# Binarised convolution, linear attention and a top-2 expert layer on one core: roots begun on ScalarE, 456 sorted chunks, a shorter Gram chain and more spread buffers

## The chip, the cores and the metric

The kernel runs on one core of a Trainium2 chip. A core has TensorE (PE in the profile; PEld are its weight loads), VectorE (DVE), ScalarE (ACT), GpSimd (POOL) and SyncE (SP), each with its own in-order stream of instructions, and 16 DMA engines that move data between device memory and the on-chip SBUF. The metric is device time of one execution, in microseconds (us), as the median of several executions.

## What is computed

The input x is 32 images of 128 channels and 56 x 56 pixels, so 3136 tokens of 128 numbers an image. Cut to what matters:

```python
# layer 0: group norm, signs, 3x3 convolution with signs as weights, scaled by channel
x = x + conv(sign(gn(x)), sign(w)) * Alpha          # w from M, Z, rv
# layer 1, on tokens t = x as (image, 3136, 128)
n = layernorm(t)
q, k, v = n @ Wq + bq, n @ Wk + bk, n @ Wv + bv
t = t + q * sum_over_tokens(k * v)                  # one row of 128 per image
n = layernorm(t)
p = softmax(n @ router_w + router_b)                # 8 experts
w1, w2 = the two largest of p, divided by their sum
t = t + w1 * (n @ E[e1] + b[e1]) + w2 * (n @ E[e2] + b[e2])
```

## The kernel before

**Tiles.** An image is 25 chunks of 128 tokens (the last has 64); four chunks are a block, so 7 blocks. x lies by channel (128 partitions x 3136) in one of three buffers `x_all`, and by token in one of three buffers `tok_all`. Convolution is nine bf16 matmuls for eight rows (L642). `to_tokens` (L667) turns it to tokens. `stats` (L682, L893) gives the sums for the variances, `var_of` and `rstd_of` (L507 to L527) the roots 1/sqrt(var) of all 25 chunks at once as a 128 x 25 tile: an integer shift and a subtraction from a constant make the first guess, and `NEWTON = 3` rounds of three DVE instructions refine it. This is done twice per image, for `r1` and `r2`.

**Attention.** sum(k * v) follows from the Gram matrix of the normalised tokens. `scaled` (ACT) and `gram` (PE, L744) build it with one more column, the sum of the tokens. Then a chain of eight steps goes back and forth: `kv_1` PE, `kv_2` DVE (three instructions), `kv_3` PE, `kv_4` DVE, `kv_5` PE (a one-column product that turns the row kv into a column), `kv_6` DVE, `kv_7` PE, `kv_8` ACT. Their results are the matrix `move` and the bias, which `project` (L863) and `bias` (L815) need.

**Experts, dense.** For a dense block the kernel computes all eight experts. The gates of the tokens (zero for six of eight) go to device memory (`gate_store`) and come back spread over 128 partitions: `spread` (L1132) loads two experts' gates for a block, 512 KB, into one of four `bc` buffers. `gated` (L1141) multiplies the turned tokens by them on DVE, and `experts` (L1159) sums the products on PE, two f32 matmuls for a `gated`. `finish` and `store` follow.

**Experts, sorted.** For the other chunks only the two chosen experts are computed. Images form groups; `GROUPS = (8, 8, 8, 4)` gives the groups' sizes and `DENSE = (8, 8, 12, 12)` the number of an image's chunks that stay dense; the last four images are dense throughout. That makes 428 sorted chunks. Each token has one of 28 pairs of experts. `pair_of` and `places` count, within the group, how many tokens of the pair came before, with the group's count so far carried as two bf16 rows `count_h` and added by two one-row matmuls (L1281). `scatter` (POOL, L1365) writes each row of a chunk to its place. When the group is complete, `list_1` to `list_4` make the list of tiles of 128 rows with one pair each. Four tiles are a quad: `tile_load` (SP), `tile_turn` (L1669), `tile_experts` (L1687, with the experts' columns from registers), `tile_read` (ACT, L1705 and L1712), `tile_sum`, `tile_out`, `tile_store`. Then `gather` (POOL, L1444) fetches rows back by token, `back_turn` (L1459), `back_out` (ACT, L1467, into one of two `o` buffers) and `back_store` (SP, L1471) finish them.

**Order.** Each step is entered with `at(due, key, engine, work, do, after, take, free, delay)`: a due time, its engine, an estimated cost, what it must follow, and which rings of buffers it takes and frees. `in_order` simulates the engines with these costs and picks, among the steps that can start soonest on an engine, the one with the earliest due time. An image begins every `P = 60` planned us. `TILE_PACE` sets over how many images' time a group's quads are due, `GATHER_PACE` the same for its gathers. The program is then emitted in that order, and each engine runs its share in it. SP issues nearly all transfers in one queue: spreads, tile loads, stores and the loads of x.

The lines that say where a spread lands before the change:

```python
bc = bpool.tile([C, 2, WIDE], F32, tag="bc", bufs=4, name=f"bc_{i}_{b}_{k}")
nc.sync.dma_start(
    bc[:, :, :n],
    d["gp"][b, 2 * k : 2 * k + 2, :n].unsqueeze(0).to_broadcast([C, 2, n]),
)
```

Of the kernel before, what the change touches and what calls it, by code (L numbers as in the profile page):

```python
# [54 lines left out]
C = 128  # L55
# [13 lines left out]
GROUPS = (8, 8, 8, 4)  # L69
DENSE = (8, 8, 12, 12)  # L70
# [9 lines left out]
NEWTON = 3  # L80
# [4 lines left out]
TILE_PACE = (0.7, 0.6, 0.4, 0.3)  # L85
GATHER_PACE = (1.0, 0.8, 0.5, 0.4)
N_Q = C + 2 * N_EXP
Q_GROUP = 3

# [10 lines left out]
    t_in=3, turned=2, v=3, w=2, back=12, sent=4, o=2,  # L100
# [85 lines left out]
def conv_attn_moe_kernel(  # L186
# [63 lines left out]
    one_i = const.tile([C, 1], I32, name="one_i")  # L250
    nc.vector.memset(one_i, 1)
    guess = const.tile([C, 1], I32, name="guess")
    nc.vector.memset(guess, 0x5F3759DF)
# [64 lines left out]
    for j in range((K_REP + 1) // 2):  # L318
        flat = tok_all[j].rearrange("p c e -> p (c e)")
        z_sb += [flat[:, : TAPS * C], flat[:, TAPS * C : 2 * TAPS * C]]  # L320
    for k in range(2):
        load_x(0, nc.sync, k, 2)
# [37 lines left out]
    wv_bk = const.tile([C, C], F32, name="wv_bk")  # L360
    n_bkbv = const.tile([C, C], F32, name="n_bkbv")
# [5 lines left out]
    def prepare():  # L367
# [25 lines left out]

        nc.vector.tensor_mul(wv_bk, wv_sb, bk_bc)
        nc.vector.scalar_tensor_tensor(
            n_bkbv, bk_bc, float(n_tok), bv_bc, ALU.mult, ALU.mult
        )

# [30 lines left out]
    count_h = const.tile([C, 2, N_PAIR], BF16, name="count_h")  # L429
# [5 lines left out]
    def prepare_sorted():  # L435
        nc.gpsimd.memset(hot_all, 0.0)
        nc.vector.memset(count_h, 0.0)
# [68 lines left out]

    def rstd_of(var, dst, name):  # L507

        square = spool.tile([C, n_ck], F32, tag=f"square{name}", bufs=1, name="square")
        shape = [C, n_ck]  # L510
        nc.vector.tensor_tensor(
            square.bitcast(I32),
            var.bitcast(I32),
            one_i.to_broadcast(shape),
            ALU.logical_shift_right,
        )
        yield
        nc.vector.tensor_tensor(
            dst.bitcast(I32), guess.to_broadcast(shape), square.bitcast(I32), ALU.subtract
        )  # L520
        for _ in range(NEWTON):
            yield
            nc.vector.tensor_mul(square, dst, dst)
            yield
            nc.vector.scalar_tensor_tensor(square, square, -0.5, var, ALU.mult, ALU.mult)
            yield
            nc.vector.scalar_tensor_tensor(dst, square, 1.5, dst, ALU.add, ALU.mult)  # L527

    def sent_from(i, g):
# [5 lines left out]
        return [("scatter", i, c) for c in blocks[g]]  # L535

# [7 lines left out]
    def plan_image(i: int):  # L544
# [144 lines left out]

        def rstd1():  # L690
            yield from rstd_of(d["var1"], d["r1"], "1")
# [34 lines left out]
        at(s + 44, ("rstd1", i), "DVE", [0.10] * (2 + 3 * NEWTON), rstd1, after=[("var1", i)])  # L726
# [33 lines left out]
        def kv_2():  # L760
            tok_sum = d["g_sb"][:, C : C + 1]
            prod = spool.tile([C, C], F32, tag="prod", bufs=1, name=f"prod_{i}")
            nc.vector.scalar_tensor_tensor(prod, bv_bc, tok_sum, d["gv"], ALU.mult, ALU.add)
            yield
            nc.vector.tensor_mul(prod, prod, wk_sb)
            yield
            nc.vector.scalar_tensor_tensor(prod, wv_bk, tok_sum, prod, ALU.mult, ALU.add)
            d["prod"] = prod

        def kv_3():  # L770
            d["kv_ps"] = ps_acc.tile([C, C], F32, tag="acc", name=f"kv_ps_{i}")
            nc.tensor.matmul(d["kv_ps"], lhsT=ones, rhs=d["prod"], start=True, stop=True)

        def kv_4():

            kv = spool.tile([C, C], F32, tag="prod", bufs=1, name=f"kv_{i}")
            nc.vector.tensor_add(kv, n_bkbv, d["kv_ps"])
# [4 lines left out]
            d["kv"] = kv  # L782

        def kv_5():
            d["kvc"] = ps_acc.tile([C, 1], F32, tag="acc", name=f"kvc_ps_{i}")
            nc.tensor.matmul(d["kvc"], lhsT=d["kv"], rhs=ident[:, :1], start=True, stop=True)
# [1091 lines left out]
```

## Time and profile before

| what | us |
|---|---|
| median of three runs (2252.52, 2253.8, 2270.36) | 2253.8 |
| the profiled execution's own time | 2270.18 |
| its span, first to last instruction | 2268.4 |
| PE busy | 2103.4 |
| DVE busy | 1970.1 |
| ACT busy | 1531.2 |
| POOL busy | 1041.1 |

The mean granted clock of PE was 0.975, the DMA engines moved 198 GB/s on average. Busy time is the time in which an engine had at least one instruction under way; matmuls overlap, so a busy PE isn't PE at its best pace. A line of a group of instructions names line, engine and operation, then what is written and read, the count, and after the bar the busy time and the mean duration in ns, then the idle time of the engine just before these instructions with what ended it. In the chain of waits each line has its start, its length and what the end of the run was waiting for. An f32 matmul shows as two records of PE, so the 384 units of `experts` with two matmuls each are 1536 records.

### The profile page before, as it was taken

The page shows a single profiled execution, that of the slowest core. Times are in us where ns is not written, and L with a number is a line of the kernel's source. Part 1 is how long each engine was busy: PE and PEld are TensorE (multiplying, and loading weights), DVE is VectorE, ACT ScalarE, POOL GpSimd, SP SyncE. Part 2 cuts the span into 40 slices and gives each one's busy share as a digit, 9 for nine tenths or more (in the row PEclk, how much of TensorE's full clock was granted, in tenths as well). Part 3 has the DMA queues.
Part 4 walks back from the last instruction along what each step waited for, and adds up shares of the span by engine and source line. Part 5 has one row for each costly group of instructions (what it writes and reads, how often), then busy time and mean ns, then how long its engine had stood idle before and what let it go on. Part 6 is the DMA issues. An engine that isn't in the chain of part 4 may idle for free.

```text
span 2268.4 us, 45320 instructions
## 1 busy us (share of the span) xinstructions
PE 2103.4 (93%) x12074; PEld 1449.1 (64%) x12074; DVE 1970.1 (87%) x6074; ACT 1531.2 (68%) x4917; POOL 1041.1 (46%) x1013
## 2 busy tenths in 40 slices
PE   5899999899999999789999999988999999999888
PEld 2666656557777776457676776655676666676544
DVE  4899999999989999688888889988898798789865
ACT  5667776668888887468777867655877776574311
POOL 3044443333433325466443644676654446233563
PEclk9989999999999999899999999999999999999999
DMA  4155544465665565377667766667767777878788
GB/s 166 30 175 177 167 153 141 138 184 184 203 186 165 176 181 168 110 219 252 194 202 220 226 198 202 215 214 240 225 195 232 217 203 247 249 214 270 222 278 273
DMA packets 324364, 448.58 MB, mean 198 GB/s; under 512 B 61832, under 2 KB 222128, under 8 KB 324112
## 3 DMA queue, kind: packets, MB, share of 16 engines
q1 hardware_dynamic: 294384, 382.80, 54.7%
q0 software_dynamic: 28144, 56.14, 8.2%
q10 hardware_dynamic: 1584, 6.75, 0.8%
q8 instruction: 102, 1.67, 0.3%
q14 instruction: 150, 1.23, 0.2%
HBM read 319.51 MB, written 126.00 MB: 196 GB/s over the span
## 4 chain that ended last, share of the span: by engine, by line
PE 42%; DVE 5%; DMA 3%; issue 2%; ACT 2%; another core or an unknown queue 1%; SPq 0%; POOL 0%; DVEq 0%; ACTq 0%; POOLq 0%
PE ff L1159 14%; PE to L1687 7%; PE cv L642 6%; PE q L863 3%; PE gram L744 3%; PE turn L1669 2%; PE back_ps L1459 2%; PE xt L667 2%; DVE gated L1141 1%; DMA back<-res,res_no 1%; PE l L1114 1%; DMA out_dram<-o 1%; PE ff L1153 1%; DMA bc<-gp 0%
## 5 line engine op out<-in xcount | busy, mean ns | idle before, releaser
L1365 POOL DMA_INDIRECT rows<-tok,row_no x428 | 524.3, 1225 | 570.5 <-ACT tok L1358 235.8
L1159 PE MATMUL ff<-gated,ew_d 128*128 128x512 f32 (+1 forms) x1536 | 711.5, 592 | 23.8 <-DVE gated L1141 19.8
L1444 POOL DMA_INDIRECT back<-res,res_no x428 | 485.4, 1134 | 464.1 <-PE back_ps L1459 264.1
L1141 DVE TENSOR_TENSOR gated<-tt,bc 128x1024 f32<-128x1024 f32 x384 | 450.7, 1180 | 92.2 <-PE ff L1159 29.9
L642 PE MATMUL cv<-xs,w_bin 128*128 128x440 bf16 (+3 forms) x2016 | 429.8, 362 | 18.5 <-ACT xs L599 10.0
L1159 PEld LDWEIGHTS ff<-gated,ew_d 128*128 128x128 f32 x1536 | 274.5, 193 | 258.6 <-issue 202.2
L1705 ACT ACTIVATE v<-to,t_in 128x128 f32<-128x128 f32 x528 | 255.3, 484 | 138.1 <-PE to L1687 74.6
L642 PEld LDWEIGHTS <-w_bin 128*128 128x128 bf16 x2016 | 200.1, 100 | 187.8 <-issue 38.3
L1687 PEld LDWEIGHTS to<-ew_s,turned 128*128 128x128 f32 x2112 | 260.8, 194 | 57.8 <-issue 32.4
L877 ACT ACTIVATE qs<-q,r 128x136 f32<-128x136 f32 (+1 forms) x800 | 247.6, 406 | 70.3 <-PE q L863 35.1
L1687 PE MATMUL to<-ew_s,turned 128*128 x2112 | 273.3, 279 | 18.2 <-ACT turned L1675 8.1
L735 ACT ACTIVATE y<-tok,r 128x128 f32<-128x128 f32 (+1 forms) x800 | 257.0, 428 | 24.3 <-PE gram L744 10.4
L863 PE MATMUL q<-move,x 128*128 128x144 f32 (+1 forms) x1600 | 239.9, 295 | 12.7 <-issue 3.7
L863 PEld LDWEIGHTS q<-move,x 128*128 128x128 f32 (+1 forms) x1600 | 213.6, 193 | 42.4 <-issue 21.1
L744 PEld LDWEIGHTS gram<-y 128*128 128x128 f32 (+1 forms) x1600 | 203.3, 192 | 53.9 <-issue 40.4
L744 PE MATMUL gram<-y 128*128 128x129 f32 (+1 forms) x1600 | 217.8, 281 | 12.9 <-issue 8.1
L682 DVE BATCH_NORM_STATS2 st<-tok 128x6 f32<-128x128 f32 (+1 forms) x800 | 185.4, 279 | 31.9 <-ACT tok L673 26.9
L1712 ACT ACTIVATE w<-to,t_in 128x128 f32<-128x128 f32 x528 | 208.6, 395 | 0.0
L893 DVE BATCH_NORM_STATS2 st<-tok 128x6 f32<-128x128 f32 (+1 forms) x800 | 198.1, 284 | 6.3
L673 ACT COPY tok<-xt 128x512 f32<-128x512 f32 (+1 forms) x224 | 121.2, 561 | 99.9 <-PE xt L667 71.6
L653 DVE SCALAR_TENSOR_TENSOR x<-cv,alpha_col,x 128x448 f32<-128x448 f32 x224 | 151.3, 676 | 40.1 <-PE cv L642 7.2
L890 DVE TENSOR_TENSOR tok<-tok,qs 128x408 f32<-128x408 f32 (+1 forms) x288 | 156.1, 542 | 29.4 <-ACT tok L882 24.1
(229 smaller groups left out, 2896.0 us busy)
## 6 DMA issues: line engine op xcount, KB each, us to landing
bc<-gp SPq DMA_DIRECT2D x368, 512.0 KB
x<-in_x_dram SPq DMA_DIRECT2D x116, 392.0 KB
t_in<-rows SPq DMA_DIRECT2D x528, 66.0 KB
res<-v SPq DMA_DIRECT2D x132, 256.0 KB
out_dram<-o SPq DMA_DIRECT2D x100, 256.0 KB
out_dram<-tt SPq DMA_DIRECT2D x92, 256.0 KB
rows<-zeros SPq DMA_DIRECT2D x116, 66.0 KB
rows<-tok,row_no POOLq DMA_INDIRECT x428
```

Of the source, the lines that this page charges most:

```text
L642: nc.tensor.matmul(cv[:, r0:r1, c0:c1], lhsT=w_bin[:, t, :], rhs=xs[:, b * ROWS + dy + r0 : b * ROWS + dy + r1, dx + c0 : dx + c1], start= ...
L735: nc.scalar.mul(y[:n, j, :C], d["tok"][:n, c, :C], d["r1"][:n, c : c + 1])
L744: nc.tensor.matmul(d["gram"], lhsT=y[:n, j, :C], rhs=y[:n, j, :], start=(c == 0), stop=(c == n_ck - 1),)
L863: nc.tensor.matmul(p[:n, k, :], lhsT=d["x"][:, c * C : c * C + n], rhs=move, start=True, stop=True,)
L877: nc.scalar.mul(qs[:n, k, :], p[:n, k, : C + N_EXP], d["r1"][:n, c : c + 1])
L1141: nc.vector.tensor_tensor(g[:, :, :n], d["tt", b][:, :n].unsqueeze(1).to_broadcast([C, 2, n]), d.pop(("bc", b, k))[:, :, :n], ALU.mult,)
L1159: nc.tensor.matmul(d["ff", b][:, :n], lhsT=ew_d[:, e * C : (e + 1) * C], rhs=g[:, j, :n], start=False, stop=(e == N_EXP - 1),)
L1365: dma = nc.gpsimd.indirect_dma_start(out=groups[group]["rows"], out_offset=bass.IndirectOffsetOnAxis(ap=d["row_no"][:n, c - n_dense : c - ...
L1444: dma = nc.gpsimd.indirect_dma_start(out=d["back", c][:n, :], out_offset=None, in_=groups[group]["res"][: quads_of(group) * WIDE, :], in_o ...
L1687: nc.tensor.matmul(p[:, k, j, :], lhsT=t[:, n * C : (n + 1) * C], rhs=ew_s[:, bass.ds(d["cols", q][j][n], C)], start=True, stop=True,)
L1705: nc.scalar.activation(d["v", q][:, n, :], p[:, k, 0, :], AF.Identity, bias=row[:, C + 2 : C + 3], scale=row[:, C : C + 1],)
L1712: nc.scalar.mul(d["w", q][:, n, :], p[:, k, 1, :], row[:, C + 1 : C + 2])
```

## The change

1. `rstd_of` starts from `seed_of`: ScalarE computes exp(-0.5 ln(var)), and one Newton round follows on DVE in place of three. New steps `seed1`, `seed2` stand on ACT between `var` and `rstd`. The set of ACT's functions that has both is loaded at the start.
2. `GROUPS` becomes (8, 8, 7, 5) and `DENSE` (8, 8, 8, 12): images 16 to 22 keep 8 dense chunks instead of 12, image 23 passes to the last group and keeps 12. 456 chunks are sorted, 139 quads instead of 132. `TILE_PACE` becomes (0.8, 0.7, 0.5, 0.4).
3. The two bf16 parts of the count stand in rows 0 and 32 of one tile, with `both` selecting these rows, so that one 33-row matmul adds them.
4. The Gram chain: the terms in the token sum are added by matmuls in `kv_3`, which also makes the column that `kv_5` made; `kv_5` is gone and `kv_6` follows `kv_3` directly.
5. In images 30 and 31 every second spread of a block sequence goes to one of three slots in the x buffer that image 29 used, once its projection is done. They count as a ring of their own, `late`.

```diff
-GROUPS = (8, 8, 8, 4)
-DENSE = (8, 8, 12, 12)
+GROUPS = (8, 8, 7, 5)
+DENSE = (8, 8, 8, 12)
...
-NEWTON = 3
...
-TILE_PACE = (0.7, 0.6, 0.4, 0.3)
+TILE_PACE = (0.8, 0.7, 0.5, 0.4)
...
+LATE, LATE_IN = 30, 29
...
+    nc.scalar.preload_act_table_set("natural_log_exp_and_others")
     for k in range(2):
         load_x(0, nc.sync, k, 2)
     nc.scalar.dma_start(rv_bc, rv.to_broadcast([C, K_REP]))
...
+    def seed_of(var, dst):
+        nc.scalar.activation(dst, var, AF.Ln)
+        nc.scalar.activation(dst, dst, AF.Exp, scale=-0.5)
+
     def rstd_of(var, dst, name):
 
         square = spool.tile([C, n_ck], F32, tag=f"square{name}", bufs=1, name="square")
-        shape = [C, n_ck]
-        nc.vector.tensor_tensor(
-            square.bitcast(I32),
-            var.bitcast(I32),
-            one_i.to_broadcast(shape),
-            ALU.logical_shift_right,
-        )
+        nc.vector.tensor_mul(square, dst, dst)
         yield
-        nc.vector.tensor_tensor(
-            dst.bitcast(I32), guess.to_broadcast(shape), square.bitcast(I32), ALU.subtract
-        )
-        for _ in range(NEWTON):
-            yield
-            nc.vector.tensor_mul(square, dst, dst)
-            yield
-            nc.vector.scalar_tensor_tensor(square, square, -0.5, var, ALU.mult, ALU.mult)
-            yield
-            nc.vector.scalar_tensor_tensor(dst, square, 1.5, dst, ALU.add, ALU.mult)
+        nc.vector.scalar_tensor_tensor(square, square, -0.5, var, ALU.mult, ALU.mult)
+        yield
+        nc.vector.scalar_tensor_tensor(dst, square, 1.5, dst, ALU.add, ALU.mult)
...
+    n_late = n_tok // (2 * WIDE)
+
+    def late_of(i, n):
+
+        turn = n % (2 * n_late + 1)
+        return turn // 2 if i >= LATE and turn % 2 else None
...
-        at(s + 44, ("rstd1", i), "DVE", [0.10] * (2 + 3 * NEWTON), rstd1, after=[("var1", i)])
+        at(s + 43, ("seed1", i), "ACT", 0.45, seed1, after=[("var1", i)])
+        at(s + 44, ("rstd1", i), "DVE", [0.10] * 3, rstd1, after=[("seed1", i)])
...
         def kv_2():
-            tok_sum = d["g_sb"][:, C : C + 1]
-            prod = spool.tile([C, C], F32, tag="prod", bufs=1, name=f"prod_{i}")
-            nc.vector.scalar_tensor_tensor(prod, bv_bc, tok_sum, d["gv"], ALU.mult, ALU.add)
-            yield
-            nc.vector.tensor_mul(prod, prod, wk_sb)
-            yield
-            nc.vector.scalar_tensor_tensor(prod, wv_bk, tok_sum, prod, ALU.mult, ALU.add)
-            d["prod"] = prod
-
-        def kv_3():
-            d["kv_ps"] = ps_acc.tile([C, C], F32, tag="acc", name=f"kv_ps_{i}")
-            nc.tensor.matmul(d["kv_ps"], lhsT=ones, rhs=d["prod"], start=True, stop=True)
+            d["prod"] = spool.tile([C, C], F32, tag="prod", bufs=1, name=f"prod_{i}")
+            nc.vector.tensor_mul(d["prod"], wk_sb, d["gv"])
+
+        def kv_3():
+            p = ps_acc.tile([C, C + 1], F32, tag="acc", name=f"kv_ps_{i}")
+            tok_sum = d["g_sb"][:, C : C + 1]
+            nc.tensor.matmul(
+                p[:, :C], lhsT=tok_sum.to_broadcast([C, C]), rhs=wv_bk, start=True, stop=False
+            )
+            nc.tensor.matmul(p[:, :C], lhsT=ones, rhs=d["prod"], start=False, stop=True)
+            nc.tensor.matmul(p[:, C:], lhsT=d["prod"], rhs=ones[:, :1], start=True, stop=False)
+            nc.tensor.matmul(p[:, C:], lhsT=wv_bk, rhs=tok_sum, start=False, stop=True)
+            d["kv_ps"] = p
...
-        def kv_5():
-            d["kvc"] = ps_acc.tile([C, 1], F32, tag="acc", name=f"kvc_ps_{i}")
-            nc.tensor.matmul(d["kvc"], lhsT=d["kv"], rhs=ident[:, :1], start=True, stop=True)
...
-            bc = bpool.tile([C, 2, WIDE], F32, tag="bc", bufs=4, name=f"bc_{i}_{b}_{k}")
+            slot = late_of(i, b * N_EXP // 2 + k)
+            if slot is None:
+                bc = bpool.tile([C, 2, WIDE], F32, tag="bc", bufs=4, name=f"bc_{i}_{b}_{k}")
+            else:
+                bc = x_all[LATE_IN % HELD][:, slot * 2 * WIDE : (slot + 1) * 2 * WIDE]
+                bc = bc.rearrange("c (j t) -> c j t", j=2)
...
             if not first_of_group:
-                for j in range(2):
-                    nc.tensor.matmul(
-                        p,
-                        lhsT=ones_h[:1],
-                        rhs=count_h[:1, j].unsqueeze(1).to_broadcast([1, n_sort + 1, N_PAIR]),
-                        start=False,
-                        stop=False,
-                    )
+                nc.tensor.matmul(
+                    p,
+                    lhsT=both,
+                    rhs=count_h.unsqueeze(1).to_broadcast([n_part, n_sort + 1, N_PAIR]),
+                    start=False,
+                    stop=False,
+                )
```

The second root (`seed2`, `rstd2`) is changed like the first, and constants are prepared once at the start: `wv_bk` takes in the term in `bv`, `rw_n` the router times the constant part of the column.

## The prediction

> **What bounds the kernel now.** I read the page's busy times first, then a table of busy time by stage, then the timelines of TensorE (PE) and VectorE (DVE), and last the chain at the end of the span.
>
> ```profile
> PE 2103.4 (93%) x12074; PEld 1449.1 (64%) x12074; DVE 1970.1 (87%) x6074; ACT 1531.2 (68%) x4917; POOL 1041.1 (46%) x1013
> L1159 PE MATMUL ff<-gated,ew_d 128*128 128x512 f32 (+1 forms) x1536 | 711.5, 592 | 23.8 <-DVE gated L1141 19.8
> L1141 DVE TENSOR_TENSOR gated<-tt,bc 128x1024 f32<-128x1024 f32 x384 | 450.7, 1180 | 92.2 <-PE ff L1159 29.9
> ```
>
> Two engines are nearly full, so the share alone decides nothing. The stages do (columns: PE, PE weight loads, DVE, ACT, POOL busy with instruction counts, granted clock, DMA share, GB/s):
>
> ```profile
> 100.00:540.00 440.00, 406.75 (x2285) 269.38 (x2284) 427.48 (x1504) 299.82 (x1007) 183.59 (x169) 0.97 0.49 155
> 540.00:900.00 360.00, 353.04 (x2277) 260.40 (x2277) 337.96 (x1065) 304.50 (x995) 136.62 (x110) 1.00 0.60 181
> 900.00:1060.00 160.00, 136.04 (x746) 90.15 (x745) 131.19 (x465) 104.21 (x342) 95.35 (x83) 0.93 0.62 196
> 1060.00:1500.00 440.00, 425.69 (x2552) 302.76 (x2550) 394.17 (x1180) 329.39 (x1057) 224.35 (x190) 0.99 0.70 214
> 1500.00:1560.00 60.00, 49.71 (x246) 30.85 (x245) 46.37 (x172) 28.29 (x92) 41.45 (x38) 0.89 0.56 157
> 1560.00:1900.00 340.00, 318.78 (x1930) 230.96 (x1930) 287.09 (x849) 248.28 (x786) 182.26 (x158) 0.98 0.76 227
> 2100.00:2268.00 168.00, 143.17 (x520) 78.41 (x519) 113.21 (x214) 32.23 (x92) 85.71 (x74) 0.93 0.79 258
> ```
>
> DVE sets the pace up to 540 us (97% busy), PE from 540 to 900 (98%) and mostly to 2100. Around 900 and 1500, where a group of sorted images turns over, and after 2100, no engine is full and PE's clock falls.
>
> Busy matmuls overlap, so I took each PE record's cost from its start to the next start, idle left out. The medians: ff 0.430 us a record (an f32 matmul is two records), to 0.112, 128-wide transposes 0.110, the bias matmul 0.22, kv_ps 0.150, a 504-wide count matmul 0.265. Median times count, over all kinds, is 2004 us of PE work at full pace. The other 264 us of the span are 27 of start, about 138 of gaps, and about 99 of slower records. The same reading prices a small DVE instruction: chained, 0.22 apart; between other work it adds only 0.08.
>
> ```profile
> 919.62 0.19 DVE L511 TENSOR_TENSOR square<-var,one_i 128x25 int32<-128x25 int32 x1
> 919.85 0.19 DVE L518 TENSOR_TENSOR r<-guess,square 128x25 int32<-128x25 int32 x1
> ...
> 911.98 0.17 DVE L525 SCALAR_TENSOR_TENSOR square<-square,var 128x25 f32<-128x25 f32 x1
> 912.06 0.29 DVE L893 BATCH_NORM_STATS2 st<-tok 128x6 f32<-128x128 f32 x1
> ```
>
> Over the run, L523, L525, L527 take 0.156, 0.152, 0.135 each and L511, L518 0.138 and 0.144; that is what I subtract, not their 180 ns of busy time.
>
> **The change, part by part.**
>
> *Roots.* 64 roots lose two integer steps and two of three Newton rounds: 128 x (0.156+0.152+0.135) + 64 x (0.138+0.144) = 74.8 us of DVE, 2.34 per image. They gain two 128x25 activations each. The nearest row is the Exp on ratio (L973, same shape, 226 ns median, 0.172 start to start): 128 x 0.172 = 22 us of ACT, in an engine 68% busy. What the trace does not show is the new trip DVE to ACT to DVE. Its nearest case is the same Exp: DVE's L977 behind it never sat idle for it in 32 cases, while ACT waited for DVE there 1.4 us on average (46.1 in 32). So the lower bound of the added wait is 0 and the upper 64 x 1.4 = 90 us of ACT idle, which matters only between 540 and 900, where ACT is 85% busy: 6 images x 2 x 1.4 = 17 us, with the seeds' own 2 us: 19. I take 3, since the tiles there are also spread out. The seeds also shorten the chain from 11 dependent steps to 5.
>
> The one ACT_TABLE_LOAD, 1.28 us at 8.15, now precedes the weight transfers on ACT's queue, whose sums release the first convolution: 0 to +1.3, I take 1. The changed kernel's instruction list has one table load, as before. The Trainium skill ("ScalarE: Activation LUTs", What ACT_TABLE_LOAD costs) speaks against mixing functions: each switch to another set is about 2.7 us. By that rule, as an estimate, two switches per root would be 128 x 2.7 = 340 us. No run here shows a second load.
>
> *Shorter Gram chain.* DVE's three steps (0.300, 0.243, 0.289) become one of about 0.21: -0.62 per image, 20 us in all. PE loses the one-column kvc matmul and gains a 128-wide and two one-column f32 ones: 0.30 + 0.16 = 0.46 per image, +15 us. One hop PE to DVE to PE disappears; in mid-run other work covers it. It shows where cover is thin: at image 31 PE idles 2.21 before L786. Bounds 0 and -2.2 at each of images 0, 1 and 31; I count it in the tail.
>
> The clock falls with such holes: between 100 and 120 us PE's gaps are at most 2.3 us long and the granted clock is 0.74. The Trainium skill ("TensorE: Matmul & The Clock Gate", What's actually happening) puts the drop to half rate after an idle window of about 3.4 us, by which holes this short should cost only themselves. The trace disagrees.
>
> *Counts.* 48 one-row matmuls become 24: -5 us of PE. A bf16 rest of one row instead of 128 on DVE changes nothing that I can price: 0.
>
> *Seven dense blocks become sorted* (428 to 456 chunks; 528 to 556 tiles, since each group also pads). A dense block costs PE 16 x 0.430 + 0.22 + 4 x 0.110 + 0.11 = 7.65: -53.6. A tile costs 0.110 + 4 x 0.112 = 0.56, so 28 are +15.6; turning 28 chunks back +3.1; wider places +1.5. Net -33 us of PE. DVE: 28 gated products at 1.11 and 7 finishes at 0.6 out, -35; tile sums +9, wider one-hot rows +7: -19. ACT: 28 x (0.346+0.260+0.329) + 3 = +29. POOL: 28 x (1.225+1.134) = +66, with about 95 us of ring waits between 1944 and 2085 to absorb it. SP's transfers: -28 spreads of 512 KB, +28 tile loads and 7 result stores.
>
> *Later tiles.* Group 0's forty quads are asked for over 6.4 images rather than 5.6, so ACT has less per image before 900 and PE something to do after it. In 900 to 1060 PE lacks 24 us; I bound the effect by -15 and +15 and take -3.
>
> *More late slots.* Images 30 and 31 get three more spread buffers. What they address is in the chain at the end:
>
> ```profile
> 2192.32 9.07 another core or an unknown queue
> 2201.43 0.04 issue
> 2201.47 0.59 ACT o L1467
> 2202.08 0.36 SPq L1471
> 2202.44 0.04 issue
> 2202.48 6.24 DMA bc<-gp
> 2208.75 1.24 DVE gated L1141
> ```
>
> ACT waits 9 us for an o buffer, the store behind it blocks SP's in-order queue, and the spread queued behind the store lands 6 us later; the clock in that slice is 0.72. With seven slots the spreads stand earlier on SP. Bound: nothing, or the 15 us from 2192 to 2208; with the Gram chain I take -8 for the tail.
>
> **The sum**, against the profiled execution's own 2270.2 us. To 540: DVE sheds 2.34 + 0.62 = 2.96 for each of nine images, 27; PE, at full pace 373 of the 420 us from 120 to 540, leaves room, but then both engines are tight: -20 (between -27 and 0). Swap, where PE is 94 to 97% busy: -28 of the 33, the rest lost in gaps (between -35 and -15). Gram matmuls less counts after 540: +7. Turnovers -3, ACT waits +3, start +1, tail -8. Total -48, that is 2222. The profiled run lies 16 above the median of the three shown (2253.8); the same difference there gives **2206**.
>
> **Rivals.**
> 1. *PE takes it all back* (about the same). If the stage to 540 is really PE's, with DVE merely running beside it, -20 becomes 0 and the seeds cost ACT 10: -18, so 2236. For it: PE is 92% busy there too. Against it: DVE's starts leave no gap at all from 200 to 400.
> 2. *The gathers at the end* (slower). From 2085 on POOL's gathers run almost without a pause, 1.25 apart, through an o ring of two whose stores land in 5.6 and 6.75 us. If the 28 more chunks all fall there, they cost 28 x 1.25 = 35, and seven more o blocks 7 x 6.75 = 47, a whole landing each as at 2180: +82 in place of -8. With the other terms as they are that gives 2254 - 48 + 90 = 2296. It decides once the last gather comes later than about the middle of image 31's dense blocks. Against it: in the changed order the last turned-back block stands behind image 31's third dense block, one block earlier than before.
> 3. *More comes back than work* (faster still). Holes cost twice, by themselves and by the clock. If a third of the 237 us of gaps and slow records goes with 114 us of DVE work: -79 and -24 of PE work, 2151.
> 4. *Tables are reloaded all the same*: 128 x 1.28 = 164 us on ACT, above 2300. One load in the list speaks against it.
>
> **How the numbers follow.** Forecast 0.60; rival 3 0.15; rival 1 0.14; rival 2 0.10; rival 4 0.01. The predicted time is 2206. A measurement of this kernel tells about 1% from no change (2231 and 2276). Faster 0.75, same 0.15, slower 0.10. The range runs from 2160, which leaves out the lower half of rival 3, to 2255, which leaves out rival 2 and takes in rival 1 and the bad bounds of the first stage and the swap.
>
> **What would show it.** Right: DVE busy about 1820 to 1860 and PE's about 2080; images before 540 us some 2 us closer together; L973-like activations of var at about 0.23 us with no idle on DVE behind them; 340 full-width gated products; no 5 us wait of gated for bc in image 31. Wrong: DVE waiting for r; ACT full from 540 to 900; PE's gaps after 2100 grown beyond 25 us with back on their releasers; a second ACT_TABLE_LOAD.

## The result, and the profile after

The changed kernel took 2284.3 us (median; 2270.3 to 2294.9) against 2262.1 for the kernel before (2252.5 to 2277.9): ratio **1.010**, 95% interval 1.005 to 1.015. It is about 1% slower; 2206 had been forecast. The profiled execution took 2278.9, its span is 2277.2. Here and below, ratios and intervals leave out executions more than 1.5% above the fastest of their kernel, medians don't, and no trace of such an execution (after_again, old_groups_again) is read.

First the page of the changed kernel: busy times and the two groups that were shown of before, then the two activations and the first of the three DVE steps of a root (a line's mean in ns stands after the bar's first number).

```profile
PE 2092.3 (92%) x12224; PEld 1469.9 (65%) x12224; DVE 1875.7 (82%) x5492; ACT 1580.9 (69%) x5136; POOL 1066.6 (47%) x1069
...
L1179 PE MATMUL ff<-gated,ew_d 128*128 128x512 f32 (+1 forms) x1424 | 658.3, 592 | 22.0 <-DVE gated L1161 19.4 <-issue 2.2
...
L1161 DVE TENSOR_TENSOR gated<-tt,bc 128x1024 f32<-128x1024 f32 (+1 forms) x332 | 391.2, 1184 | 134.6 <-PE ff L1179 41.7 <-remote 21.9 <-issue 16.9
```

```profile
L518 ACT ACTIVATE r<-var 128x25 f32<-128x25 f32 x64 | 15.9, 249 | 15.6 <-DVE var L515 14.0 <-issue 1.3 <-DVE gated L1161 0.3
L519 ACT ACTIVATE r<-r 128x25 f32<-128x25 f32 x64 | 14.4, 225 | 2.0
L524 DVE TENSOR_TENSOR square<-r 128x25 f32<-128x25 f32 x64 | 11.7, 182 | 13.8 <-ACT r L519 6.0 <-issue 5.0 <-ACT r L518 2.6
```

The work went nearly as forecast: DVE is busy 94 us less, PE's matmuls at their median pitch sum to 1975 us in place of 1999 (one set of medians for both; the prediction's grouping gave 2004), a seed's two activations take 0.25 and 0.23 us, DVE waits 8.6 us in all for them. What didn't go as forecast is in the stages (columns as in the prediction's table):

```profile
100.00:540.00 440.00, 413.46 (x2390) 281.50 (x2390) 420.77 (x1400) 321.92 (x1088) 186.69 (x177) 0.98 0.50 163
540.00:900.00 360.00, 355.70 (x2324) 265.53 (x2323) 330.06 (x979) 311.97 (x1037) 122.07 (x101) 1.00 0.62 184
900.00:1060.00 160.00, 137.60 (x761) 94.75 (x760) 122.60 (x393) 103.30 (x336) 92.17 (x84) 0.90 0.56 171
1060.00:1500.00 440.00, 401.61 (x2495) 292.29 (x2494) 360.19 (x1104) 330.52 (x1082) 250.65 (x216) 0.95 0.62 185
```

From 1060 to 1500, where PE had been 97% busy at a clock of 0.99, it is 91% busy at 0.95. Counted as PE work still to do, after against before, the changed kernel leads by 37 us at 540, 51 at 1000, 40 at 1300, 32 at 1400, 5 at 1500, and is 18 behind at 2100; 23 of the lead is work that no longer exists. So about 50 us were won by 1000 and lost again, most of it before 1500.

**What PE waits for there.** The timeline of PE in the changed kernel (start, length, what ran, and in brackets the idle time before it with its releaser):

```profile
1038.56 0.27 PE L756 MATMUL gram<-y 128*128 128x129 f32 x1 [0.85 <-issue]
1039.30 0.35 PE L756 MATMUL gram<-y 128*128 128x129 f32 x1 [0.48 <-issue]
1040.70 0.37 PE L756 MATMUL gram<-y 128*128 128x129 f32 x1 [1.05 <-issue]
1042.13 0.38 PE L756 MATMUL gram<-y 128*128 128x129 f32 x1 [1.05 <-issue]
...
1048.47 0.37 PE L1695 MATMUL turn<-ident,t_in 128*128 128x128 f32 x1 [1.72 <-issue]
1049.87 0.58 PE L1695 MATMUL turn<-ident,t_in 128*128 128x128 f32 x2 [1.03 <-issue]
```

"issue" means that nothing in the profile explains the wait. These matmuls come 0.11 apart elsewhere; here PE takes its instructions one by one at multiples of 0.70 us. I call this a **hold**. POOL meanwhile issues one gather after another, eleven in a row, 1.25 apart but for one step of 2.0:

```profile
1040.06 0.95 POOL L1470 DMA_INDIRECT back<-res,res_no  x1 [0.30 <-issue]
1041.32 0.95 POOL L1470 DMA_INDIRECT back<-res,res_no  x1 [0.31 <-issue]
1042.57 0.96 POOL L1470 DMA_INDIRECT back<-res,res_no  x1 [0.30 <-issue]
```

Summed over the run, PE's idle time that ends on "issue" is 32.9 us in the first profile of before and 43.3 in that of after. The kernel before has such a hold between 924 and 943 us, in the stage that the prediction passed over as "no engine is full":

```profile
939.75 0.37 PE L744 MATMUL gram<-y 128*128 128x129 f32 x1 [2.53 <-issue]
941.16 0.38 PE L744 MATMUL gram<-y 128*128 128x129 f32 x1 [1.04 <-issue]
942.57 0.37 PE L744 MATMUL gram<-y 128*128 128x129 f32 x1 [1.03 <-issue]
```

### The profile page after: what moved, and what is told of

Same layout as the page of the kernel before. It is cut to its first block, busy times and chain, and to the rows that moved or that the text cites. A ratio compares the mean times of both kernels' runs of the same rounds, so it can differ in the third digit from the quotient of the medians.

```text
span 2277.2 us, 45445 instructions
## 1 busy us (share of the span) xinstructions
PE 2092.3 (92%) x12224; PEld 1469.9 (65%) x12224; DVE 1875.7 (82%) x5492; ACT 1580.9 (69%) x5136; POOL 1066.6 (47%) x1069
## 5 line engine op out<-in xcount | busy, mean ns | idle before, releaser
L1391 POOL DMA_INDIRECT rows<-tok,row_no x456 | 535.5, 1174 | 621.5 <-ACT tok L1384 364.9
L1470 POOL DMA_INDIRECT back<-res,res_no x456 | 500.8, 1098 | 381.0 <-PE back_ps L1485 162.4
L1179 PE MATMUL ff<-gated,ew_d 128*128 128x512 f32 (+1 forms) x1424 | 658.3, 592 | 22.0 <-DVE gated L1161 19.4
L1161 DVE TENSOR_TENSOR gated<-tt,bc 128x1024 f32<-128x1024 f32 (+1 forms) x332 | 391.2, 1184 | 134.6 <-PE ff L1179 41.7
L1179 PEld LDWEIGHTS ff<-gated,ew_d 128*128 128x128 f32 x1424 | 255.9, 193 | 241.4 <-issue 195.2
L1731 ACT ACTIVATE v<-to,t_in 128x128 f32<-128x128 f32 x556 | 263.8, 475 | 166.5 <-PE to L1713 60.7
L1713 PEld LDWEIGHTS to<-ew_s,turned 128*128 128x128 f32 x2224 | 276.3, 196 | 62.0 <-issue 35.2
L1713 PE MATMUL to<-ew_s,turned 128*128 x2224 | 290.7, 281 | 25.9 <-ACT turned L1701 13.1
L690 DVE BATCH_NORM_STATS2 st<-tok 128x6 f32<-128x128 f32 (+1 forms) x800 | 182.9, 276 | 40.1 <-ACT tok L681 32.3
L904 DVE BATCH_NORM_STATS2 st<-tok 128x6 f32<-128x128 f32 (+1 forms) x800 | 191.4, 283 | 7.4
L1384 ACT ACTIVATE tok<-tok,a 128x128 f32<-128x128 f32 (+1 forms) x456 | 172.4, 432 | 0.3
```

What stands on the lines that cost most here:

```text
L1161: nc.vector.tensor_tensor(g[:, :, :n], d["tt", b][:, :n].unsqueeze(1).to_broadcast([C, 2, n]), d.pop(("bc", b, k))[:, :, :n], ALU.mult,)
L1179: nc.tensor.matmul(d["ff", b][:, :n], lhsT=ew_d[:, e * C : (e + 1) * C], rhs=g[:, j, :n], start=False, stop=(e == N_EXP - 1),)
L1391: dma = nc.gpsimd.indirect_dma_start(out=groups[group]["rows"], out_offset=bass.IndirectOffsetOnAxis(ap=d["row_no"][:n, c - n_dense : c - ...
L1470: dma = nc.gpsimd.indirect_dma_start(out=d["back", c][:n, :], out_offset=None, in_=groups[group]["res"][: quads_of(group) * WIDE, :], in_o ...
L1713: nc.tensor.matmul(p[:, k, j, :], lhsT=t[:, n * C : (n + 1) * C], rhs=ew_s[:, bass.ds(d["cols", q][j][n], C)], start=True, stop=True,)
L1731: nc.scalar.activation(d["v", q][:, n, :], p[:, k, 0, :], AF.Identity, bias=row[:, C + 2 : C + 3], scale=row[:, C : C + 1],)
```

## The experiments

The theories. **A**: the new turnover loses (narrow: the later tiles crowd it; wide: the group of seven; in both, SP's queue stuck behind a result store, 21.9 us near 1392 in the profile after). **B**: the planner's order falls well or badly, whatever is changed. **C**: the trip of the roots or the Gram chain costs. **D**: the holds are the chip's, not the kernel's. **E**: on such a chip gathers without a pause bring the holds. Kernels measured together ran on one chip, and their ratios are to the kernel before on that chip.

**Parts of the change, on chip 2.** The kernel before takes 2175.8 there.

old_groups is the changed kernel with the first six lines below, old_pace the same kernel with the two of TILE_PACE alone, groups_only the kernel before with the first six turned round, and nudge_before the kernel before with the last two.

```diff
-GROUPS = (8, 8, 7, 5)
+GROUPS = (8, 8, 8, 4)
-DENSE = (8, 8, 8, 12)
+DENSE = (8, 8, 12, 12)
-TILE_PACE = (0.8, 0.7, 0.5, 0.4)
+TILE_PACE = (0.7, 0.6, 0.4, 0.3)
...
-GATE_LANDS, SPREAD_LANDS, STORE_LANDS, TILE_LANDS, GATHER_LANDS = 5.0, 6.5, 5.0, 6.0, 12.0
+GATE_LANDS, SPREAD_LANDS, STORE_LANDS, TILE_LANDS, GATHER_LANDS = 5.0, 6.6, 5.0, 6.0, 12.0
```

> The changed kernel with the groups, the dense counts and the pace of the tiles put back, so that roots, Gram chain, counts and late slots are changed alone. Theory A (the regrouping made the turnover near 1400 us that lost 40 us in the changed kernel's trace): this keeps what the two traces show won before 1060 us, some 35 to 50 us, and is 2205 to 2225, ratio 0.975 to 0.985 against the kernel before. Theory B (the written order happens to fall well or badly, whatever part moves it): anywhere within 1.5% of the kernel before, about 2230 to 2290, with its losses at a place of its own. Theory C (the roots' trip to ScalarE or the Gram chain is what costs): as slow as the changed kernel, ratio about 1.01.

> The kernel before with only the groups, the dense counts and the pace of the tiles changed. Theory A: slower than the kernel before, ratio 1.01 to 1.02 (2280 to 2305), because the 33 us of TensorE's work that it saves are lost together with another 20 to 40 at the turnover of the group of seven, with the fall of TensorE's busy share between 1380 and 1510 us. Theory B: within 1.5% either way, with no fixed place. Theory C: faster by the swap's own 28 us, ratio about 0.988.

> The changed kernel with the pace of the tiles alone put back. In the planner's times this moves the end of the first group's gathers 48 us earlier, away from the first tile stores of the third group. Theory A in its narrow form (the later tiles push the old group's gathers and result stores into the turnover): 30 to 45 us faster than the changed kernel, ratio 0.98 to 0.99, and no wait of some 20 us of SP for an o store near 1400 us. Theory A in its wide form (the group of seven itself): as the changed kernel, 1.005 to 1.015. Theory B: within 1.5% of the kernel before.

> The kernel before with one planned duration, that of a spread's landing, put at 6.6 in place of 6.5, which changes the written order of the instructions and nothing else. Theory B: the time moves by 10 us or more, up or down. Theories A and C: it stays within 0.4% of the kernel before.

| on chip 2 | us | ratio, interval | PE idle on "issue" |
|---|---|---|---|
| old_groups | 2153.0 | 0.989, 0.988 to 0.991 | 0.7 |
| groups_only | 2151.8 | 0.988, 0.987 to 0.990 | 0.0 |
| old_pace | 2148.9 | 0.987, 0.984 to 0.989 | 0.9 |
| nudge_before | 2185.1 | 1.004, 1.003 to 1.006 | 1.3 |

Here everything is faster. Either half brings 23 to 24 us and both with the old pace 27: the halves share one limit, since PE is 95 to 96% busy with any of them. This one change of the order is worth 9 us (B). And there are no holds. That was a reason to look at the chip, theory D.

**The change again, the roots alone, SP's queue: chip 5.** The kernel before takes 2262.4 here.

o_store_act is the changed kernel with the edit below. roots_only is the kernel before with `seed_of`, `rstd_of`, `seed1`, `seed2` and the loading of the set of functions as in the changed one. after_again and before_again are unchanged.

```diff
-            nc.sync.dma_start(
+            nc.scalar.dma_start(
                 out[i].rearrange("c h w -> c (h w)")[:, lo:hi], d.pop(("o", b))[:, : hi - lo]
...
-                due + each * k / n_sort + 8, ("back_store", i, b), "SP", 0.43, back_store, b,
+                due + each * k / n_sort + 8, ("back_store", i, b), "ACT", 0.1, back_store, b,
```

> The changed kernel as it is, on the chip of the runs before this. Theory D (the executions compared first had TensorE held where it waited for nothing that the profile shows: 32.9 us of such idle before, 43.3 us after, but 0 to 1.3 us in the four kernels since): here such idle is below 3 us and the changed kernel is faster than the kernel before, ratio 0.985 to 0.992 (2143 to 2158 where the kernel before takes 2176). Theory A (the turnover of the group of seven with the later tiles loses what is won): still slower, ratio 1.005 to 1.015, with SP held some 20 us by one o store near 1400 us while the version with the old pace is not. Theory B (luck of the order): anywhere from 0.985 to 1.01, without such idle.

> The kernel before with the roots begun on ScalarE and nothing else changed. The prediction's own steps give 9 images of 2.34 us less DVE before 540, that is 15 to 20 us, 3 us of new waits, 1 of the table: 12 to 18 faster, ratio about 0.993. If PE sets the pace of that stage all the same: 0.997 to 1.002. If the new trip costs what the nearest row allows (19 us and more): slower, 1.002 to 1.008.

> The changed kernel with the stores of the turned-back blocks issued by ScalarE, right behind its copy, in place of SP, where they stand ahead of spreads and tile loads. Theory A: these stores no longer hold SP's queue; 10 to 25 us faster than the changed kernel in the same call. Theories B and D: within 6 us of it.

> The kernel before as it is, for its trace beside the others of this chip. Theory D: idle of TensorE that ends on nothing shown is below 3 us in place of 32.9, the clock is 0.98 or more in place of 0.975, and the span 2170 to 2184. Otherwise it is as in the first profile, 2252 to 2278.

These runs fell on chip 5, while D's forecasts were for chip 2. after_again 2281.0, ratio 1.006 (1.003 to 1.010); roots_only 2279.3, 1.008 (1.005 to 1.011); o_store_act 2288.2, 1.015 (1.008 to 1.022); before_again 2269.1 in one run, with 39.1 us of "issue" idle. So on this chip the kernel before has the holds too, as in the first comparison (D). SP's stuck queue, the best mark of A, isn't the cause: without these stores in it the kernel is no faster (1.015 against 1.006, in intervals that overlap). The roots alone miss their forecast. In the first stage PE then has four holes for `gated` (one line of its waits from 240 to 480 us in roots_only, then the same line in before_again):

```profile
PE ff L1159 <- DVE gated L1141: 12.7, 4, 3.2
```

```profile
PE ff L1159 <- DVE gated L1141: 1.9, 5, 0.7
```

From image 4 to image 8 an image took 51.7 us in place of 49.6, and image 9 came 8 us later (an image is dated by its last `scaled` step, and the first is image 0). That the new order left these holes is likely, not shown: nudge_before, where the order alone is new, has 51.5 us an image there. But DVE also waits 13.4 us for the seeds in roots_only (8.6 in the changed kernel), so that theory C has a part in the loss of the roots alone isn't excluded.

**The same kernel on two kinds of chip.** The stages of groups_only, first on chip 2, then, as groups_only_again, on chip 12:

```profile
1060.00:1500.00 440.00, 426.55 (x2751) 315.92 (x2750) 411.25 (x1331) 367.78 (x1196) 294.61 (x249) 0.98 0.71 217
1500.00:1900.00 400.00, 392.81 (x2370) 283.82 (x2368) 355.29 (x980) 299.43 (x942) 241.91 (x209) 1.00 0.82 248
```

```profile
1060.00:1500.00 440.00, 394.40 (x2392) 284.87 (x2391) 354.74 (x1144) 320.19 (x1032) 238.85 (x205) 0.94 0.58 177
1500.00:1900.00 400.00, 354.03 (x2130) 256.37 (x2129) 318.93 (x951) 277.00 (x887) 205.77 (x186) 0.96 0.68 199
```

> The kernel before with the regrouping and the pace alone, once more. If the regrouping is the part that loses where TensorE is held in runs of gathers (it had 221 gathers in long runs on the chip without holds, the kernel before with the nudge 131): on such a chip slower than the kernel before, ratio 1.005 to 1.025, with idle of TensorE that ends on nothing shown above 45 us, where it gained 1.2% on the chip without holds. If the other parts together with it make the loss: 0.985 to 1.0.

> The changed kernel with the old pace of the tiles, once more. Theory A in its narrow form (the later tiles are what costs where TensorE is held): on such a chip 15 to 40 us faster than the changed kernel, ratio 0.985 to 0.998. Theory E alone: it has as many gathers and bunches them as much, so within 10 us of the changed kernel there, 1.0 to 1.01. On the chip without holds 0.987 as before.

> Roots, Gram chain, counts and late slots without the regrouping, once more. If the regrouping brought the loss where TensorE is held: on such a chip it keeps part of its 23 us, ratio 0.985 to 0.997. If less work for DVE is enough to bring the gathers closer together (the roots alone had 118 gathers in long runs, where the kernel before has 72): 1.0 to 1.01. On the chip without holds 0.989 as before.

| | chip 2 | a chip with holds |
|---|---|---|
| kernel before | 2175.8 | 2262 to 2283 |
| regrouping and pace alone | 0.988 | 2305.2, **1.017** (1.011 to 1.023), chip 12 |
| all but these | 0.989 | 2248.1, **0.983** (0.976 to 0.990), chip 13 |
| changed kernel, old pace | 0.987 | 2321.1, 1.016 (1.009 to 1.024), chip 13 |
| changed kernel | not seen | 1.006 (chip 5), 1.005 (chip 13), 1.010 (first) |

This settles which half loses: the regrouping gains some 24 us on chip 2 and loses some 40 on chip 12; the rest gains on chips 2 and 13. B alone can't be the cause, since groups_only runs in the same order on both chips. The narrow form of A is probably wrong in sign: on chip 13 the later tiles go with a faster regrouped kernel (1.016 to 1.005, in two comparisons). E had forecast no difference there (1.0 to 1.01) and missed too. The changed kernel itself was never seen on chip 2, and it did not run beside old_pace_again and the others that were compared with 2283.0 on chip 13; its ratios in three comparisons are 1.005 to 1.010.

The two traces of groups_only part where the gathers begin. The first gather starts at 910.3 us on chip 2 and at 918.9 on chip 12, 9 us apart; the ends are 164 apart.

The traces differ in one more thing. Most transfers in chip 2's traces leave 16 marks on their semaphore as they land. Counting 16 for each, chip 2's four traces hold 96 to 97% of the marks, all the others 52 to 70%, and the lack begins with the first images. A wait whose mark is missing also counts as "issue". Before the first gather, 0.7 to 7.8 us of PE's idle time count so in the traces that lack marks, and 0.0 to 0.7 in chip 2's. So some of each sum of "issue" may be ordinary waiting. The pitch of 0.70 us and the times from start to start don't depend on marks. Every execution here comes with a recorded span and clock; whether the recording has a part in the holds, no run shows.

A look at eight microseconds of the same gathers, in the changed kernel of the first comparison and in groups_only on chip 2, shows what a hold does (POOL issues 5 to 7 of them in each stretch, the fifth count):

```profile
1036.00:1044.00 8.00, 3.87 (x22) 2.93 (x20) 6.92 (x19) 1.24 (x4) 6.17 (x7) 0.76 0.20 52
1044.00:1052.00 8.00, 2.23 (x8) 1.62 (x8) 0.00 (x0) 0.40 (x1) 4.59 (x5) 0.50 0.20 50
```

```profile
1032.00:1040.00 8.00, 8.00 (x55) 6.02 (x54) 7.65 (x23) 6.24 (x21) 5.93 (x6) 1.00 0.46 104
1040.00:1048.00 8.00, 8.00 (x54) 5.08 (x54) 7.96 (x36) 6.77 (x23) 5.87 (x6) 1.00 0.54 135
```

PE does 8 matmuls in place of 54, DVE and ACT run dry behind it, and the clock falls to 0.50, though no gap of PE is longer than 1.72 us. The Trainium skill ("TensorE: Matmul & The Clock Gate", What's actually happening) lets the clock fall after an idle window of some 3.4 us. This trace shows it fall under many shorter gaps.

To see how far this goes with POOL, I took for each matmul the time to the next start beyond the median of its kind as lost, from 860 to 2100 us, by how many gathers POOL began in the 8 us before:

| share of PE's time lost | 0 gathers | 1, 2 | 3, 4 | 5 or more | us in the last class |
|---|---|---|---|---|---|
| before, first profile | 5% | 10% | 13% | 21% | 37 of 175 |
| after, first profile | 8% | 13% | 13% | 33% | 78 of 239 |
| groups_only, chip 12 | 11% | 14% | 17% | 31% | 75 of 240 |
| groups_only, chip 2 | 7% | 6% | 8% | 8% | 25 of 333 |
| old_pace, chip 13 | 9% | 13% | 17% | 39% | 91 of 234 |
| old_pace, chip 2 | 4% | 7% | 9% | 8% | 26 of 331 |

On chip 2 dense gathers cost nothing special. In the other traces PE loses 21 to 39% of its time beside them, and the change has more of them: of the 57 us more that after loses (196 against 139), 41 are in the last class.

**Spacing the gathers.** If E is right, gathers with a pause between them bring no holds. after_spaced is the changed kernel with the edit below; after_spaced_twice has six fillings, before_spaced the three in the kernel before; space_first_group and old_groups_spaced_first have them with `group == 0` alone, the latter in old_groups; nop_before_gather has one `nc.gpsimd.nop()` in their place; after_third is unchanged.

```diff
+    filler = const.tile([C, C], F32, name="filler")
...
         def gather(c):
             d["back", c] = bpool.tile([C, C], F32, tag="back", bufs=14, name=f"back_{i}_{c}")
             n = rows_of(c)
+            for _ in range(3):
+                nc.gpsimd.memset(filler, 0.0)
```

> The changed kernel as it is, as the yardstick of this call. Theory E (on one of the two chips seen so far, runs of six and more gathers of POOL without a pause hold TensorE: 25 of 87 us of such runs lost in the kernel before, 87 of 161 in the changed one; on the other chip 7 to 10% of them): on the first kind of chip ratio 1.005 to 1.015 against the kernel before, with over 50 us of TensorE's time lost in such runs; on the second kind 0.985 to 0.992, with less than 30. Theory A (the turnover of the group of seven in itself): slower on either.

> The changed kernel with three small fillings of a spare tile on POOL ahead of each gather (some 0.6 us, nothing else altered), so that gathers come about 1.9 us apart in place of 1.26. Theory E: on the chip that holds TensorE half or more of the loss goes, 30 to 60 us faster than the changed kernel in this call; on the other chip within 8 us of it. Theory A or any cause in the order: within 8 us of it on either, or slower, since gathers only come later.

> The same with six fillings, gathers about 2.5 us apart. Theory E: on the chip that holds TensorE at least as fast as with three, unless POOL itself is late by then (456 gathers by 1.2 us are 550 us more of POOL, 73% busy in all): 30 to 70 us faster than the changed kernel; on the other chip 0 to 20 slower. Theory A: slower on either.

> The kernel before with three fillings ahead of each gather. Theory E: on the chip that holds TensorE 10 to 25 us faster than the kernel before, since it has 25 us to lose in such runs; on the other within 8 us. Theory A: within 8 us on either.

On chip 13 (before 2266.5): after_third 2278.6, 1.005 (1.002 to 1.009); after_spaced 2347.0, 1.034 (1.027 to 1.040); after_spaced_twice 2673.0, 1.179 (1.172 to 1.186); before_spaced 2303.6, 1.015 (1.009 to 1.022). In time the expectations of E for the three spaced kernels failed. With three fillings the gathers come 2.20 us apart and not 1.9 as planned. In the traces E's first half stands: "issue" idle of PE falls from 47.9 us to 10.7 in the changed kernel and from 39.1 (chip 5) to 13.3 in the kernel before. By image 22 the spaced version is 26 us ahead of after_third (1316.5 against 1343.0); 8 of these it had at image 16 (906.8 against 914.7), where the gathers begin. Then POOL is late and PE, in order, waits for gathers; the page of after_spaced, and a line of PE's waits from 1390 to 1510:

```profile
PE 2102.8 (90%) x12224; PEld 1474.6 (63%) x12224; DVE 1876.8 (80%) x5492; ACT 1587.8 (68%) x5136; POOL 1368.0 (58%) x2437
```

```profile
PE back_ps L1488 <- DMA back<-res,res_no: 25.0, 7, 13.2
```

So spacing took most of the "issue" idle away and put another wait in its place.

> The changed kernel with the three fillings ahead of the gathers of the first group alone (136 of 456), so that POOL isn't late at the end. Theory E: on a chip that holds TensorE in runs of gathers, some 25 us of such holds go between 900 and 1450 us, as they did with all gathers spaced, and none is given back at the end: 15 to 35 us faster than the changed kernel on such a chip (2279), ratio 0.99 to 1.0 against the kernel before. If what spacing gained up to image 23 was only gathers put off: no faster, 1.003 to 1.012. On a chip without holds: within 8 us of the changed kernel.

> The changed kernel with one empty POOL instruction ahead of each gather, as each scatter has one: runs of scatters, as close as those of gathers, lost next to nothing. If the empty instruction is what spares TensorE there: as fast as with the first group spaced, or faster, 20 to 45 us below the changed kernel, with under 25 us of idle that ends on nothing shown. If it is that gathers read device memory where scatters write it: within 8 us of the changed kernel, the idle unchanged at 40 to 70.

> Roots, Gram chain, counts and late slots without the regrouping, with three fillings ahead of the gathers of the first group. Theory E (holds come from gathers without a pause): on a chip with holds 5 to 20 us faster than the same without fillings (0.983), ratio 0.972 to 0.981. If the spacing of the first group gains nothing of its own: 0.982 to 0.99. On the chip without holds 0.987 to 0.993, as without fillings.

space_first_group 2279.7, 0.998 (0.994 to 1.002, chip 13, before 2283.0); nop_before_gather, beside it, 2314.9, 1.016 (1.009 to 1.023); old_groups_spaced_first 2240.6, 0.989 (0.984 to 0.994, chip 12, before 2264.1). Against the kernel before, spacing where POOL has room takes about 0.7% off the changed kernel on this chip (1.005 to 0.998, between two comparisons whose intervals touch). That is weak: the changed kernel had 2278.6 without it, and it is the kernel before that took 16.6 us longer in the second comparison. In the trace the spacing works where it was put: "issue" idle of PE between 900 and 1450 us is 7.9 in place of 26.1 (after_third). An empty instruction doesn't help, with 56.9 us of "issue" idle; that it costs 1% I can't explain. Without the regrouping the spacing adds nothing that can be seen (0.989 on one chip, 0.983 without it on another).

**What is settled.** The regrouping is the half that loses on the chips with holds. Holds come beside gathers issued without a pause, and with spaced gathers most of the "issue" idle goes. **What stays open**: what in the chip holds PE, and why one chip doesn't; and that the holds are what the regrouping pays for is argued from traces, since no spaced version of the changed kernel was clearly faster than the changed kernel. Nor do the holds account for the whole: groups_only loses 77 us more than the kernel before from 860 to 2100 (216 against 139), 38 of them in the class of five or more gathers. The other 39 are spread over the rest of the stage, partly as waits that follow a hold; that they all do isn't shown.

In the first comparison most of the lead goes between 1300 and 1500 us, and of PE's 20.5 us of idle time from 1350 to 1500 (3.7 before) only 1.9 end on "issue". First the stage before, then after, then PE's longest waits after:

```profile
1350.00:1500.00 150.00, 146.32 (x809) 96.73 (x808) 142.55 (x450) 106.23 (x344) 90.65 (x73) 1.00 0.70 228
```

```profile
1350.00:1500.00 150.00, 129.27 (x742) 88.97 (x741) 118.07 (x386) 92.01 (x302) 85.28 (x78) 0.92 0.55 168
PE xt L675 <- DVE x L661: 6.4, 1, 6.4
PE gram L756 <- ACT y L747: 4.1, 2, 3.7
PE gv L770 <- ACT g_sb L766: 2.7, 1, 2.7
PE list_ps L1669 <- DVE vals L1662: 2.0, 1, 2.0
PE gram L756 <- issue: 1.9, 2, 1.6
```

On chip 2 groups_only's lead over nudge_before (the kernel before but for its order), counted as above, also falls there, from 38 us at 1300 to 24 at 1500, and is 33 again at 1600. So the turnover of the group of seven, the wide form of A, may have a part in the loss; no run tests it apart from the holds.

**Faster than both** is old_groups, the change without its second part: 0.989 on chip 2, 0.983 on chip 13.

## Why the prediction was wrong

**The step that failed is the swap** ("Seven dense blocks become sorted", -28, with -3 for the turnovers). Its PE work was sized well: where nothing holds PE, the regrouping gives some 24 us. On a chip with holds it costs some 40. What the step left out, as far as the runs show it, is what 28 more gathers do beside PE. It priced them at 66 us of POOL "to absorb" in ring waits, as if an engine with time to spare could only hurt by being late. POOL's busy time rose by 25 us only; PE lost 78 us beside its dense gathers in place of 37. The rest of the loss, at the turnover of the new group and after it, stays open.

**It could have been seen.** The prediction's table had 900 to 1060 with no engine full and the clock at 0.93, and it asked only what the change adds there. PE's waits in that trace end on "issue" for 32.9 us, all but 5 of them after the first gather. A stage in which no engine is full has an unknown limit, and a change that adds POOL work to it can't be costed at nothing. Why gathers bunch more in the changed kernel is only argued: POOL's scatters wait longer for ACT's rows, and the gathers queued behind them then go without a pause. The waits of POOL, before and after:

```profile
L1365 POOL DMA_INDIRECT rows<-tok,row_no x428 | 524.3, 1225 | 570.5 <-ACT tok L1358 235.8
```

```profile
L1391 POOL DMA_INDIRECT rows<-tok,row_no x456 | 535.5, 1174 | 621.5 <-ACT tok L1384 364.9 <-issue 88.6 <-DVE gt_parts L1066 27.9
```

**The other terms.**

| step | forecast | seen |
|---|---|---|
| roots and Gram chain, DVE | -74.8 and -20 us of DVE | DVE busy -94 with the swap's share, where 114 was summed |
| wait for the seeds | 3 us | 8.6 us of DVE idle |
| stage to 540 | -20 | image 9 comes 7.5 us earlier, image 16 27 earlier; the roots alone 8 later |
| later tiles | -3, within 15 | some -25 on chip 13 (1.016 to 1.005, in two comparisons), outside the bounds |
| tail | -8 | from image 31's last scaled chunk to the end 145.5 in place of 159.2: -14; waits of `gated` for `bc` 1.3 us after 2130 |
| the sum | parts add | they don't: -23 and -24 give -27 on chip 2 |

Leaving aside the 23 us of work that is gone, the lead was 14 us at 540, where 20 had been forecast, and 28 at 1000; so the first part came smaller and later, and was there at 1000 us. That it and the swap can simply be added was wrong even without holds. The likely reason is that DVE's relief and the swap both end on PE, which has only so many gaps to give back (it is 95 to 96% busy on chip 2).

**The rivals.** PE taking it all back (2236) and more coming back (2151) didn't happen. The slower rival named 2296, near the outcome, and the right engine, but another mechanism: it had the gathers late at the end, so that its number came near is luck. The last one came at 2233.6, 13 us after image 31's first `gated`, no later than before (2241.1), and PE's gaps after 2100 are about 13 us. The tables weren't reloaded. The range to 2255 had no room for what no term stood for, a cost on PE of work on POOL.

## What to carry to other kernels

Where PE's idle time ends on "issue" and not on another engine, find out what runs beside it before adding to that work, however idle the engine that does it. Look at one kernel on more than one chip before trusting a difference of 1%: here the same edit was 1.2% faster on one and 1.7% slower on another. Count what a trace should hold before reading "issue": with up to half of the marks missing, some of it can be an ordinary wait. And gains on two engines that end at the same third one needn't add.

## What the runs showed of the hardware

I hadn't expected the same instructions to take 2176 us on one chip and 2262 to 2283 on others, with the difference in how PE takes its instructions (0.70 us each in a hold, against 0.11) and not in how long a transfer or a matmul lasts. In groups_only's traces from chip 2 and chip 12 the gathers take 4.8 and 5.2 us from their start to their landing at the median, the spreads 5.8 and 5.9 (of those transfers with all 16 marks, few on chip 12), and a record of `ff` 592 ns on both.

Runs of scatters with as short a pause between them as the gathers' (0.3 us) cost PE far less in the two traces of the kernel before: 6 and 7 us in 145 and 140, where runs of gathers cost 32 and 35 in 132 and 114 (six or more in a row). The scatters start 1.6 us apart and the gathers 1.4, so this doesn't tell whether the direction or the pace spares PE.
